# One activation function for all eight FFNs: tanh instead of Silu in four of them, in a hand-planned transformer block

## The chip, the cores and the metric

The kernel runs on one core of one Trainium2 chip. The metric is the device time of one execution in microseconds (us); before the change the median of ten runs is 2534.17 us (2533.23 to 2541.55). The engines are TensorE (PE; its weight loads are listed apart as PEld), VectorE (DVE), ScalarE (ACT), GpSimd (POOL) and SyncE (SP), which issues most DMAs.

## The reference

The input x has 4 sequences of 512 rows of 512 numbers. Four blocks follow each other, each with a layernorm in front and a residual sum behind:

1. attention A: pairwise similarities between all 512 x 512 rows by a small network with two relu layers; the 51 most similar rows are kept for each row; a softmax attention of 32 heads of size 2 over those rows
2. an FFN: `h = silu(gate) * up`, with 2048 gate and 2048 up columns, then a product back to 512
3. attention B: a "difference" attention of 16 heads over all rows, with softmax and projection
4. the same FFN again, with the same weights

`silu(g) = g * sigmoid(g)`, which is the same as `g/2 * (1 + tanh(g/2))`.

## The kernel before, in words

**Work.** The letter and digit in a tile's name tell block and sequence. *Pairs*: for each pair group (1024 in all) DVE, and in a few groups ACT, makes two tiles `m` (line 751 on), PE multiplies them by the second layer's weights into a PSUM bank `z` with 64 columns, ACT takes the relu into `r`, and PE sums over the third layer with 32 columns into `sim` (line 787). For each 128 rows `topk_tile` (line 809) finds the 51 best columns on DVE, gathers their rows with DMAs from POOL, and does the softmax with one large exponential on ACT (`sc`). *FFNs*: f0 to f3 are block 2, e0 to e3 block 4 of the four sequences. `ffn` (line 931) splits float32 into two float16 halves, so that each product is three float16 matmuls. It works in 16 chunks of 128 columns: 24 matmuls give gate and up in two PSUM banks (`e0z` and so on); an activation on ACT and multiplies on DVE give a tile `t`; ACT and DVE split it into two float16 parts for the first 256 rows (`ha`) and the last 256 (`hb`). `ha` goes into the down product at once (`e0a`). `hb` is spilled to HBM (`hk`) and fetched again later (`hc`), when the second half of the down product (`e0b`) runs with its weights `we`. *Attention B* (b0 to b3, line 1017) uses the exponential on ACT for scores and weights.

**The activation before.** Four FFNs (f0, f1, e0, e1) use Silu with a scale column, and one DVE multiply with a scale column. The other four use Tanh and two DVE multiplies with constants. Silu is in another activation table than Exp and Tanh, so a table load stands wherever the two kinds alternate.

**The order.** No instruction is issued while the code above runs: each call of an engine is recorded as a task (`Plan.add`, line 221). `Plan.issue` (line 363) then lists all tasks with a price for each (`cost`, line 148), and a forward and backward pass over the dependencies, the buffers and the engines (`run`, line 261) fixes the order on each engine. In a last pass a shift is added to the rank of each task, by the part of the work that it belongs to (table `SHIFT`, line 53, and `part`, line 73): "e2b" is the late half of e2's down product, "s33" the sums of sequence 3's last 128 rows, "p33v" half of their pair groups. All instructions are issued at line 411, so the profile shows that one line for nearly everything, and work is told by its tiles' names. PSUM has eight banks: seven of the tag `z`, shared by the pair groups, the FFNs and attention B, and one for `sim`. The buffers of tag `fh` (`ha`, `hb`, `hc`) are five.

**The stages.** Pairs of sequence 0 with the preparation of weights; then pairs of 1 to 3 beside f0, b0, e0, f1, b1, e1 and f2 (line 1242); when the pairs are done, b2 beside f3, then b3 and e3 beside e2 (lines 1243 to 1245).

Of the kernel before, what the change touches and what calls it, by code (L numbers as in the profile page):

```python
# [16 lines left out]
AF = mybir.ActivationFunctionType  # L17
ALU = mybir.AluOpType
# [26 lines left out]
def _size(dt):  # L45
# [5 lines left out]


SHIFT = {
    "X0": -16, "X1": -43, "X2": -35, "X3": -35, "a0": -71, "a1": -41, "a2": -39, "a3": -48, "b0n": 10,
    "b0p": -2, "b0q": 16, "b0s": -14, "b0t": -19, "b1n": -40, "b1p": -36, "b1q": -1, "b1s": -34, "b1t": -37,
    "b2n": 13, "b2q": 16, "b2s": -19, "b2t": -20, "b3n": -17, "b3p": 17, "b3q": -9, "b3s": -25, "b3t": -16,
    "c": -67, "e0a": 36, "e0b": 37, "e0n": 18, "e0u": 22, "e0v": 18, "e1a": -13, "e1b": 31, "e1n": -39,
    "e1u": -27, "e1v": -30, "e2a": 25, "e2b": 439, "e2n": -8, "e2u": -11, "e2v": 15, "e3a": 351, "e3b": 380,
    "e3n": 27, "e3u": 63, "e3v": 260, "f0a": 7, "f0b": 4, "f0n": 21, "f0u": 32, "f1a": -14, "f1n": -36,
    "f1u": -19, "f1v": -33, "f2a": 26, "f2b": 13, "f2n": 27, "f2u": 22, "f2v": 20, "f3a": -18, "f3b": -21,  # L60
    "f3n": -39, "f3u": -48, "f3v": -29, "k00": 13, "k01": 24, "k02": 26, "k03": 12, "k10": 50, "k11": 104,
    "k12": 66, "k13": 25, "k20": 28, "k21": 20, "k22": 19, "k23": 76, "k30": 54, "k31": 59, "k32": 70,
    "k33": 84, "p00u": -9, "p00v": -10, "p01u": 17, "p01v": 16, "p02u": 9, "p02v": 7, "p03u": 6, "p03v": 6,
    "p10u": 6, "p10v": 10, "p11u": 3, "p11v": 6, "p12u": -2, "p12v": -1, "p13u": 10, "p13v": 10, "p20u": 8,
    "p20v": 6, "p21u": -1, "p21v": -3, "p22v": -9, "p23u": -18, "p23v": 17, "p30u": 6, "p30v": 3, "p31u": -11,
    "p31v": -9, "p32u": -6, "p32v": 5, "p33u": 8, "p33v": 49, "q0": -17, "q1": 49, "q2": -87, "q3": -94,
    "s00": -358, "s01": -310, "s02": -192, "s03": -207, "s10": -196, "s11": -177, "s12": -37, "s13": 6,
    "s20": 2, "s21": -7, "s22": -2, "s23": 15, "s30": 1, "s31": -13, "s32": -14, "s33": 5, "w": 84, "y0": -82,
    "y1": 272, "y2": -299, "y3": -48,
}  # L70


# [34 lines left out]
class Plan:  # L107
# [9 lines left out]
    DRAIN = 0.1  # L117
    BUSY = 8.0
    READY, MADE = 0.185, 0.17
    LOAD = 1.3  # L120
    PERIOD = 3.41333
    LAG = {"PE": 0.2, "ACT": 0.135, "DVE": 0.12, "POOL": 0.06, "SP": 0.1}

# [24 lines left out]
    def cost(self, key, op, a, k):  # L148


        free = self.free
        if key == "PE":
            n, m = free(a[0]), free(a[1])
            f32 = a[1].dtype == F32
            if op == "transpose":
                return n / 1200 + 0.0025, 128, 0
            w = 32 if m <= 32 else 64 if m <= 64 else 128
            t = (n / 1200 + 0.0027) * 2 if f32 else n / 2400 + 0.0027
            if w < 128:
                t += 0.024 if f32 else 0.012  # L160
            return t, w, (a[0].start_partition() or 0) // w if w < 128 else 0
        if key == "SP":
            return 0.48, 0, 0
        aps = [x for x in a if hasattr(x, "tensor")]
        n = max(free(x) for x in aps)
        ptrs = sum(free(x) == 1 for x in list(a[1:]) + list(k.values()) if hasattr(x, "tensor"))
        psum = any(x.space == PSUM for x in aps)
        if key == "ACT":
            if op == "copy":
                t = 0.04 if psum else 0.08 + (0.29 if n > 600 else 0)  # L170
            elif "accum_out" in k:
                t = 0.33 if psum or n < 100 else 0.187
            else:
                t = 0.16 + (0.04 if ptrs >= 2 else 0.0) if psum else 0.185 + (0.04 if ptrs >= 2 else 0.0 if ptrs else -0.09)

            func = next((x for x in a[1:] if isinstance(x, AF)), None)
            return t + n / 1200, 0, 1 if func in (AF.Exp, AF.Tanh) else 2 if func == AF.Silu else 0
        elif key == "DVE":
            fast = op in ("tensor_scalar", "tensor_copy") and not psum
            if op == "reciprocal":  # L180
                t = 0.055 + n * 0.0064
            elif op in ("max_index", "match_replace"):
                t = 0.673
            elif op == "bn_aggr":
                t = 0.095
            elif op == "tensor_reduce" and not psum and list(a[1].ap)[-1][0] != 1:
                t = 0.06 + n * 0.00173
            elif fast and n == 1:
                t = 0.125 if ptrs >= 2 else 0.065
            else:  # L190
                t = 0.07 + n / (1920 if fast else 960)
                t += 0.06 * (ptrs if fast else op == "scalar_tensor_tensor" and ptrs > 0)
        elif op == "memset":
            t = 0.07 + n / 1200
        else:
            t = {"indirect_dma_start": 1.25, "affine_select": 0.4, "partition_all_reduce": 0.5, "tensor_tensor": 0.3 + 0.2 * n}[op]
        return t, 0, 0
# [63 lines left out]
    def run(self, rank, edges, pre, tags, back=False, stick=0.0):  # L261


        tasks = self.tasks
        n = len(tasks)
# [5 lines left out]
        start = [0.0] * n  # L271
        freed = {m: 0.0 for m in self.tiles}
        now = {k: 0.0 for k in self.kinds}
# [5 lines left out]
            if not waits[i]:  # L279
                heapq.heappush(soon[tasks[i][0]], (0.0, i))  # L280
        order = []
        mode, cols, alle, table = 128, {}, 0.0, None
        win, busy, upto, slow = 0, 0.0, 0.0, False
        P = self.PERIOD

# [16 lines left out]
        while len(order) < n:  # L302
            best = None
            for k in self.kinds:
                if k == "PE" and any(wide.values()) or k != "PE" and able[k]:
                    t = now[k]
# [6 lines left out]
            t, k = best  # L313
# [28 lines left out]
            else:  # L342
                i = heapq.heappop(able[k])[1]
                end = now[k] = t + tasks[i][7]
                if tasks[i][9] and tasks[i][9] != table:
                    if table is not None and not back:
                        end = now[k] = end + self.LOAD
                    table = tasks[i][9]
                if self.xfer[i] and not back:
                    queue = max(queue, t + 1.35) + self.xfer[i]  # L350
                    end = max(queue, t + 1.6 + 1.5 * self.xfer[i])
# [63 lines left out]
def hybrid_block(ctx: ExitStack, tc: tile.TileContext, I, out):  # L415
# [62 lines left out]
    ipw = const("ipw", [128, 5])  # L478
    sc = const("sc", [128, 16])
    s_gu, s_d, s_a, s_p, s_w = (sc[:, i : i + 1] for i in range(5))  # L480
    c_tanh, c_down, c_exp, c_proj, c_kv, w_up, w_dn, c_nexp, c_gate, c_up, c_iexp = (sc[:, i : i + 1] for i in range(5, 16))
    w2s = const("w2s", [128, 2, 64], F16)

    def top(dst, src, n):
# [62 lines left out]
    def prep_scales():  # L547
# [18 lines left out]
            V.tensor_scalar(sc[:, k : k + 1], ipw[:, k : k + 1], 2.0 ** e, None, ALU.mult)  # L566
        p = [pw[:, i : i + 1] for i in range(4)]
        V.tensor_scalar(c_tanh, p[0], 2.0 ** -20, None, ALU.mult)
        V.tensor_scalar(c_gate, p[0], 2.0 ** -19, None, ALU.mult)
        V.tensor_scalar(c_up, ipw[:, 0:1], 2.0 ** -15, None, ALU.mult)  # L570
        V.tensor_scalar(c_down, p[0], p[0], 2.0 ** -16, ALU.mult, ALU.mult)
        V.tensor_scalar(c_down, c_down, p[1], None, ALU.mult)
        V.tensor_scalar(c_proj, p[2], p[3], 2.0 ** -21, ALU.mult, ALU.mult)
# [354 lines left out]
    PARTS = ((0, 0), (0, 1), (1, 0))  # L928


    def ffn(name, X, first=False, late=False, silu=False, store=lambda t: None):
        xt = yield from normed_t(name, X)
        H = S // 2

# [25 lines left out]
        for c in range(NC):  # L960
# [21 lines left out]
                    yield 0.86  # L982
                gu.append(z)
            t = fp.tile([128, S], F32, name=f"{name}t{c}", tag="ft", bufs=2)
            if silu:
                A.activation(t, gu[0], AF.Silu, scale=c_gate)
                V.scalar_tensor_tensor(t, gu[1], c_up, t, ALU.mult, ALU.mult)
            else:

                A.activation(t, gu[0], AF.Tanh, scale=c_tanh)  # L990
                V.scalar_tensor_tensor(t, t, 1.0, gu[0], ALU.add, ALU.mult)
                V.scalar_tensor_tensor(t, gu[1], 2.0 ** -35, t, ALU.mult, ALU.mult)
            ha, hb = (fp.tile([128, 2, H], F16, name=f"{name}h{p}{c}", tag="fh", bufs=FH) for p in "ab")
            for h, ts_ in ((ha, slice(0, H)), (hb, slice(H, S))):
                A.copy(h[:, 0, :], t[:, ts_])
# [169 lines left out]
    def weave(*parts):  # L1165

        at = [p[2] for p in parts]
        live = set(range(len(parts)))
        while live:
            i = min(live, key=lambda j: (at[j], j))  # L1170
            c = next(parts[i][0], None)
            if c is None:
                live.discard(i)
            else:
                at[i] += c / parts[i][1]
                yield c
# [33 lines left out]
    def store(b, t):  # L1210
        SP.dma_start(out[b, t * 128 : (t + 1) * 128], X[b][:, t, :])
# [3 lines left out]
    def start(b):  # L1215
        step_topks(b)
        X[b] = yield from out_a(b)

    def f1(b, **kw):
        return lambda: ffn(f"f{b}", X[b], **kw)  # L1220

    def at(b, **kw):
        return lambda: attn_b(f"b{b}", X[b], **kw)

    def f2(b):
        def g():
            yield from ffn(f"e{b}", X[b], late=b > 1, silu=b < 2, store=lambda t: store(b, t))
        return g

    warm_up()  # L1230
# [4 lines left out]
    main = serial(lambda: pairs(1), lambda: pairs(2), lambda: pairs(3))  # L1235
    side = serial(
        lambda: start(0),
        lambda: weave((f1(0, first=True, silu=True)(), 1, 0), (phase_a(2), 0.2, 20)),
        at(0, first=True),
        lambda: weave((f2(0)(), 1, 0), (phase_a(3), 0.2, 20)),  # L1240
        lambda: start(1), f1(1, silu=True), at(1), f2(1), lambda: start(2), f1(2, late=True))
    emit(weave((main, 1, 0), (side, 1.8, 120)))
    emit(start(3))
    emit(weave((at(2, late=True)(), 1, 0), (f1(3, late=True)(), 1, 20)))
# [57 lines left out]
```

## Time and profile before

| what | us |
|---|---|
| median of ten runs | 2534.17 |
| the profiled execution | 2537.89 |
| its span, first to last instruction | 2536.2 |
| PE busy (records of matmuls) | 2501.5 |
| DVE busy | 2009.4 |
| ACT busy | 1514.3 |
| POOL busy | 976.9 |
| ACT table loads, 19 of 1.283 | 24.4 |
| matmuls of f0's gate and up, first to last start | 503.1 to 657.0 |
| the same of e0, f1, e1 | 980.6 to 1160.7, 1169.1 to 1345.9, 1643.0 to 1779.4 |
| the same of f2, f3, e2, e3 | 1829.0 to 1945.5, 1953.3 to 2128.0, 2222.5 to 2379.6, 2380.5 to 2485.2 |
| pair groups' matmuls, first to last start | 32.9 to 1811.0 |

Times within the span are counted from its first instruction. A line of the list of groups gives engine, operation, what is written and read, the number of instructions, their busy time and the mean of one in ns, and then the idle time of the engine in front of them and who ended it. The granted clock of PE is 0.999 of full speed over the span.

### The profile page before, as it was taken

Reading aid. Unit: us, or ns where it says so; the run is one execution under the profiler, and the core shown is the slowest. Engines: PE = TensorE matmul, PEld = TensorE weight load, DVE = VectorE, ACT = ScalarE, POOL = GpSimd, SP = SyncE. Lnnn points to the kernel's source line nnn. Section 1 sums busy time; section 2 is a strip of 40 time slices with the busy share of each in tenths; the row PEclk is TensorE's granted clock in tenths of the full one; section 3 lists DMA queues with packets and bytes.
Section 4 is the critical chain, followed back from the end, with each engine's and each line's share of the span. In section 5 each row is a group of like instructions: output and inputs, shape, how many; then the busy total and the mean of one; then the engine's idle time right before and its main releaser. Section 6 shows DMA issues by size and latency. Waiting matters only on the chain.

```text
span 2536.2 us, 42662 instructions
## 1 busy us (share of the span) xinstructions
PE 2501.5 (99%) x15044; PEld 1025.5 (40%) x15044; DVE 2009.4 (79%) x5164; ACT 1514.3 (60%) x2831; POOL 976.9 (39%) x847
## 2 busy tenths in 40 slices
PE   8999999999999999999999999999999999999998
PEld 4433343444343334444444333344444443443443
DVE  8889999999899999798686899977856555673531
ACT  6999998656458976443343689643422376586220
POOL 0277767475534155666624234465560000000000
PEclk9999999999999999999999999999999999999999
DMA  5533321157642022436535421045665535523446
GB/s 182 157 105 88 101 61 35 54 162 242 219 133 61 28 64 91 117 115 203 165 94 158 119 55 43 22 115 148 205 212 176 156 115 177 150 93 122 132 143 197
DMA packets 223628, 317.79 MB, mean 125 GB/s; under 512 B 29969, under 2 KB 150865, under 8 KB 222390
## 3 DMA queue, kind: packets, MB, share of 16 engines
q1 hardware_dynamic: 197302, 261.54, 33.1%
q0 software_dynamic: 26112, 53.53, 8.0%
q8 instruction: 118, 1.93, 0.3%
q14 instruction: 96, 0.79, 0.1%
HBM read 263.43 MB, written 51.39 MB: 124 GB/s over the span
## 4 chain that ended last, share of the span: by engine, by line
PE 74%; DVE 17%; DMA 5%; issue 2%; POOL 1%; ACT 1%; SPq 0%; DVEq 0%; POOLq 0%; ACTq 0%
PE z L411 19%; DVE m L411 8%; PE sim L411 6%; PE e0z L411 3%; PE e1z L411 3%; PE e2z L411 3%; PE e3z L411 3%; PE f3z L411 3%; PE f1z L411 3%; PE f2z L411 3%; DVE g L411 3%; PE f0z L411 2%; DVE b1s L411 1%; POOL g L411 1%; DVE b0s L411 1%
## 5 line engine op out<-in xcount | busy, mean ns | idle before, releaser
L411 DVE TENSOR_SCALAR m<-hw 128x512 f32<-128x512 f32 x1888 | 809.0, 482 | 60.6 <-PE z L411 59.5
L411 PE MATMUL z<-m,w2s 128*64 128x512 f16 x5664 | 750.1, 391 | 3.1 <-DVE m L411 1.7
L411 ACT ACTIVATE r<-z,zb 128x512 f32<-128x512 f32 x944 | 612.7, 697 | 221.3 <-PE z L411 159.4
L411 POOL DMA_INDIRECT g<-kv,ix x432 | 497.1, 1151 | 359.7 <-DVE ix L411 208.8
L411 POOL DMA_INDIRECT g<-kv,idx x384 | 469.0, 1221 | 412.7 <-DVE idx L411 194.1
L411 PEld LDWEIGHTS <-w2s 128*64 128x64 f16 x5688 | 315.8, 108 | 491.5 <-issue 226.8
L411 PE MATMUL sim<-r,w 128*32 128x512 f32 x2048 | 274.8, 604 | 0.0
L411 ACT ACTIVATE m<-h 128x512 f32<-128x512 f32 x160 | 107.9, 743 | 5.4 <-PE z L411 5.4
L411 PE MATMUL f3z<-f3xt,f3w 128*128 128x512 f16 x384 | 103.0, 379 | 0.1
L411 PE MATMUL e2z<-e2xt,e2w 128*128 128x512 f16 x384 | 101.5, 379 | 0.0
L411 PE MATMUL f2z<-f2xt,f2w 128*128 128x512 f16 x384 | 98.5, 379 | 0.5 <-DMA f2w<-wf 0.5
L411 PE MATMUL z<-m,h 128*64 128x512 f32 x320 | 98.7, 594 | 0.0
L411 DVE TENSOR_TENSOR g<-g,sc 128x832 f32<-128x832 f32 (+3 forms) x128 | 98.2, 780 | 0.3
L411 PE MATMUL f1z<-f1xt,f1w 128*128 128x512 f16 x384 | 98.3, 379 | 0.0
L411 PE MATMUL f0z<-f0xt,f0w 128*128 128x512 f16 x384 | 90.8, 379 | 0.5 <-ACT f0w L411 0.5
L411 PE MATMUL e0z<-e0xt,e0w 128*128 128x512 f16 x384 | 90.9, 379 | 0.0
L411 PE MATMUL e1z<-e1xt,e1w 128*128 128x512 f16 x384 | 89.5, 379 | 0.0
L411 PEld LDWEIGHTS sim<-r,w 128*32 128x32 f32 x2048 | 41.6, 108 | 115.9 <-issue 95.8
L411 PE MATMUL e3z<-e3xt,e3w 128*128 128x512 f16 x384 | 85.7, 379 | 0.0
L411 DVE MAX8 vm<-sims 128x8 f32<-128x512 f32 x112 | 76.6, 684 | 3.4 <-POOL sims L411 2.9
L411 DVE FIND_INDEX8 ix<-vm,sims 128x8 uint32<-128x512 f32 x112 | 76.3, 681 | 0.0
L411 DVE TENSOR_TENSOR g<-g,q 128x832 f32<-128x832 f32 x64 | 63.9, 999 | 7.1 <-DMA g<-kv,ix 6.1
(643 smaller groups left out, 3776.1 us busy)
## 6 DMA issues: line engine op xcount, KB each, us to landing
f0wr<-wf SPq DMA_DIRECT2D x48, 256.0 KB
wn<-wgu SPq DMA_DIRECT2D x32, 256.0 KB
wf<-f0w SPq DMA_DIRECT2D x16, 512.0 KB
e0w<-wf SPq DMA_DIRECT2D x16, 512.0 KB
f1w<-wf SPq DMA_DIRECT2D x16, 512.0 KB
e1w<-wf SPq DMA_DIRECT2D x16, 512.0 KB
f2w<-wf SPq DMA_DIRECT2D x16, 512.0 KB
f3w<-wf SPq DMA_DIRECT2D x16, 512.0 KB
```

Of the source, the lines that this page charges most:

```text
L411: getattr(eng, op)(*a, **k)
```

## The change

All eight FFNs use the form with Tanh. The two scale columns of the Silu form go. In the planner, the price of a table load goes, with the note of each activation's table. The table of shifts is a new one; since it sets the order of everything, all engines' orders differ, though the matmuls, DMAs and all instructions but those named here are the same in number.

```
 SHIFT = {
-    "X0": -16, "X1": -43, "X2": -35, "X3": -35, "a0": -71, "a1": -41, "a2": -39, "a3": -48, "b0n": 10,
...
+    "X0": -32, "X1": 1, "X2": -17, "X3": 1, "a0": -50, "a1": 75, "a2": -68, "a3": -47, "b0n": -7, "b0p": -12,
...
-    LOAD = 1.3
...
-            func = next((x for x in a[1:] if isinstance(x, AF)), None)
-            return t + n / 1200, 0, 1 if func in (AF.Exp, AF.Tanh) else 2 if func == AF.Silu else 0
+            t += n / 1200
...
-                if tasks[i][9] and tasks[i][9] != table:
-                    if table is not None and not back:
-                        end = now[k] = end + self.LOAD
-                    table = tasks[i][9]
...
-        V.tensor_scalar(c_gate, p[0], 2.0 ** -19, None, ALU.mult)
-        V.tensor_scalar(c_up, ipw[:, 0:1], 2.0 ** -15, None, ALU.mult)
...
-            if silu:
-                A.activation(t, gu[0], AF.Silu, scale=c_gate)
-                V.scalar_tensor_tensor(t, gu[1], c_up, t, ALU.mult, ALU.mult)
-            else:
-
-                A.activation(t, gu[0], AF.Tanh, scale=c_tanh)
-                V.scalar_tensor_tensor(t, t, 1.0, gu[0], ALU.add, ALU.mult)
-                V.scalar_tensor_tensor(t, gu[1], 2.0 ** -35, t, ALU.mult, ALU.mult)
+            A.activation(t, gu[0], AF.Tanh, scale=c_tanh)
+            V.scalar_tensor_tensor(t, t, 1.0, gu[0], ALU.add, ALU.mult)
+            V.scalar_tensor_tensor(t, gu[1], 2.0 ** -35, t, ALU.mult, ALU.mult)
...
-            yield from ffn(f"e{b}", X[b], late=b > 1, silu=b < 2, store=lambda t: store(b, t))
+            yield from ffn(f"e{b}", X[b], late=b > 1, store=lambda t: store(b, t))
...
-        lambda: weave((f1(0, first=True, silu=True)(), 1, 0), (phase_a(2), 0.2, 20)),
+        lambda: weave((f1(0, first=True)(), 1, 0), (phase_a(2), 0.2, 20)),
...
-        lambda: start(1), f1(1, silu=True), at(1), f2(1), lambda: start(2), f1(2, late=True))
+        lambda: start(1), f1(1), at(1), f2(1), lambda: start(2), f1(2, late=True))
```

Some of the shifts that the prediction touches: "e2b" goes from 439 to 46, "e3a" from 351 to 66, "e3b" from 380 to 187, "e3v" from 260 to 46, "s00" from -358 to -691, "s12" from -37 to -6.

## The prediction

> **What bounds the kernel now.** First the page: what each engine does over the whole span, then the slices.
>
> ```profile
> PE 2501.5 (99%) x15044; PEld 1025.5 (40%) x15044; DVE 2009.4 (79%) x5164; ACT 1514.3 (60%) x2831; POOL 976.9 (39%) x847
> ...
> PE   8999999999999999999999999999999999999998
> ...
> DVE  8889999999899999798686899977856555673531
> ACT  6999998656458976443343689643422376586220
> ```
>
> TensorE (PE) looks full, but a record of a matmul lasts longer than its share of the array: the records of one FFN matmul are 379 ns long, and 24 of them in a row take 5.18 us, 0.216 us each. So I price matmuls by the distance of their starts: 0.216 us for a 128x512 f16 matmul, 0.108 for one of a pair group (two column halves work side by side), 0.108 for a record of the pair sums, and so on. All matmuls of the program are then 2317 us of work in a span of 2536.2. The other 219 us are lost. The Trainium skill says the same in "Perfetto Trace Analysis", Identifying the Most-Contended Engine: matmul busy time is a poor measure of the distance to the limit. By that page's other measure, weight loads, PE would be 40% full; no row here supports a reserve that large, and nothing below rests on it.
>
> Next I cut the span where the last pair group ends, at 1811 us, and cut the part before it by stage. The columns are the stretch, its length, and the busy time of PE, weight loads, DVE, ACT and POOL.
>
> ```profile
> 0.00:1811.00 1811.00, 1786.59 (x11593) 710.71 (x11593) 1634.72 (x4215) 1198.32 (x2152) 922.14 (x795) 1.00 0.38 113
> 1811.00:2537.00 726.00, 714.87 (x3454) 314.77 (x3453) 374.69 (x949) 315.97 (x681) 54.76 (x52) 1.00 0.51 156
> ...
> 500.00:660.00 160.00, 159.21 (x914) 65.75 (x914) 146.94 (x329) 93.16 (x157) 97.43 (x80) 1.00 0.65 203
> 980.00:1162.00 182.00, 182.00 (x1104) 74.64 (x1100) 162.71 (x405) 85.21 (x143) 115.90 (x91) 1.00 0.37 111
> 1169.00:1347.00 178.00, 177.27 (x1024) 73.17 (x1023) 129.73 (x288) 69.01 (x113) 79.38 (x76) 1.00 0.50 153
> 1643.00:1781.00 138.00, 138.00 (x780) 58.22 (x780) 105.01 (x237) 53.35 (x93) 85.66 (x76) 1.00 0.44 130
> ```
>
> Before 1811 us PE does 1616.5 us of work (89%) and DVE is busy for 90%; behind it PE does 700.5 us of work in 725 (97%) and DVE is half idle. The last four rows are the stages of the four Silu FFNs (f0, e0, f1, e1): DVE idles there for 13, 19, 48 and 33 us. Between them, at 200 to 520, 760 to 1040 and 1440 to 1640 us, DVE is busy for 319 of 320, 279 of 280 and 199 of 200 us. So PE with its losses is the bound, and DVE is a second one in those three stretches. ACT ends little of the chain of waits (1%).
>
> What is PE's loss made of? Between pair groups (64 columns), pair sums (32) and everything else (128) PE changes its column width. The list of PE's instructions, by start and length:
>
> ```profile
> 1699.26 1.46 PE L411 MATMUL e1a<-e1wd,e1ha 128*128 128x512 f16 x6
> 1700.65 4.26 PE L411 MATMUL z<-m,w2s 128*64 128x512 f16 x36
> 1704.84 5.35 PE L411 MATMUL e1z<-e1xt,e1w 128*128 128x512 f16 x24
> ...
> 1711.33 0.38 PE L411 MATMUL e1z<-e1xt,e1w 128*128 128x512 f16 x1
> 1711.64 1.06 PE L411 MATMUL sim<-r,w 128*32 128x512 f32 x8
> 1712.64 3.63 PE L411 MATMUL e1z<-e1xt,e1w 128*128 128x512 f16 x16
> ```
>
> Six e1a matmuls are 1.30 us, but 1.39 pass until z starts: 0.09 for 128 to 64. 36 z are 3.89 us, 4.19 pass: 0.30 for 64 to 128. In the same way 128 to 32 costs 0.31 - 0.22 = 0.09, and 32 to 128 costs 1.00 - 0.87 = 0.13.
>
> **The change part by part.**
>
> *The order.* No matmul comes or goes. Counting the width changes in the issued order of both programs gives 936 before and 904 after: 7 fewer from 128 to 64, 3 from 64 to 128, 4 from 64 to 32, 11 from 32 to 128, 7 from 128 to 32. By the rows: 14 x 0.09 + 3 x 0.30 + 11 x 0.13 + 4 x 0.30 (64 to 32 has no row of its own; I take its dearest neighbour) = 4.8 us less. Ends: all at 0.09, 2.9; all at 0.30, 9.6.
>
> *The tail.* In the order of before, the late half of FFN e2 (e2b) runs together with that of e3 (e3b) at the end, and both fetch weights and spilled activations at once.
>
> ```profile
> 2485.39 3.19 PE L411 MATMUL e2b<-e2we,e2hc 128*128 128x512 f16 x14
> ...
> 2492.84 1.47 PE L411 MATMUL e2b<-e2we,e2hc 128*128 128x512 f16 x6 [0.81 <-DMA e2hc<-e2hk]
> 2495.33 4.92 PE L411 MATMUL e2b<-e2we,e2hc 128*128 128x512 f16 x22 [1.02 <-DMA e2hc<-e2hk]
> ```
>
> From 2485.4, when e3z is done, 192 matmuls (41.5 us) take until 2532.0: 5.1 us are lost, and the DMA engines are 98% busy at 2492 to 2500. In the new order e2b is done long before; behind e3z stand 30 e3a and 96 e3b, 27.2 us. Their first fetch (e3hc0) stands in SP's queue behind the last spill (e3hk15). In before that spill was issued 2.5 us after e3z, the next fetch 0.6 later, and PE had it 4.2 us after that: 7.3 in all, of which the 30 e3a cover 6.5. So 0.8 is left to wait and about 4 us are won. Ends: 5.1 won; or 4.0 more lost, which is what the f0b matmuls waited for DMAs.
>
> *DVE.* In 64 chunks one multiply with a scale column (0.746 us, rows of e0t to f1t) becomes two without (0.688 each, rows of e2t to f3t): 0.63 x 64 = 40 us more, 10.1 in each FFN. In f1 and e1 the idle 48 and 33 us hide it. In f0 10.1 meets 13 idle, and e0's first 60 us lie in a full stretch (about 5 of 16 chunks, 3 us). I take 4. Ends: 0, and all 40. Two dropped one-column scales are nothing.
>
> *ACT.* Tanh lasts as long as Silu (0.69 us, rows of e0t and e2t). 18 of 19 table loads go.
>
> ```profile
> 1819.33 0.58 ACT L411 CAST f2xt<-f2t 128x512 f16<-128x512 f32 x1 [4.44 <-PE f2t L411]
> 1819.93 1.28 ACT L411 ACT_TABLE_LOAD   x1
> 1821.23 1.56 ACT L411 ACTIVATE sc<-sc 128x1632 f32<-128x1632 f32 x1
> ```
>
> That is 18 x 1.28 = 23 us of ACT, which is 60% busy and about half busy where the loads stand. I take 1 us won; ends 0 and 23. The Trainium skill ("ScalarE: Activation LUTs", What ACT_TABLE_LOAD costs) adds a drain of about 1.38 us to each load; by it ACT would win 48 us. The rows show 0.02 us on either side of the load and no drain, so the rows decide.
>
> *PSUM.* The gate's bank is now held through a DVE multiply behind the activation, and the up bank for one multiply more: some 0.8 us per chunk, out of seven banks that the pair groups share. Before shows Tanh FFNs only where no pair group is left. Ends: 0, and 64 x 0.8 = 51 us; I take 1, as PE ran e3z at 105 us busy of 105 in that form.
>
> Sum: -4.8 - 4 + 4 - 1 + 1 = -4.8, so 5 us less. The profiled execution took 2537.89 us (span 2536.2) and would take 2533; it lies 3.7 over the median, so against 2534.17 I forecast **2529**.
>
> **The rivals.**
>
> *A: DVE becomes the bound until the pairs end (slower).* In the new order the last pair group stands after 1579 us of PE work, 37 earlier, with the same pair work and up to 40 us more on DVE. So DVE has 1675 us to do where PE alone would need about 1811 - 37 - 5 = 1769: a share of 94.7%, against 90.3% now. Behind the pairs there are 738 us of work, at 725/700.5 and less the tail's 4: 760. At a share of 94% the sum is 1782 + 760 = 2542, at 93% 1801 + 760 = 2561; it is slower than now below 94.4%. For it: it must nearly reach over 1800 us what only the full stretches show. Against: those three stretches, 800 us together, show 99.6%, and the idle time is in the FFN stages, where the new work is.
>
> *B: the new order fills PE better (faster).* Before the pairs end PE loses 194 us; 856 width changes at 0.15, between the prices above, are 128. The other 66 are waits. If the order saves a quarter, 16 us, the time is 2513. I cut both orders at every 59th pair group and took for each piece the larger of PE's work with 0.2 per width change and DVE's work: before's pieces come out to about 3 us, and the new order is 2 us shorter; with longer and shorter pieces between 14 shorter and 16 longer. So A and B are both open.
>
> *C: nothing.* The saved changes of width were time in which DVE caught up, and the tail waits elsewhere: 2534.
>
> **How the numbers follow.** Forecast (2522 to 2536) 0.50, of it 0.27 faster, 0.22 same, 0.01 slower; A 0.27 (0.25 slower, 0.02 same); B 0.15 faster; C 0.08 (0.05 same, 0.03 slower). Within 0.2% means within 5.1 us, about what measuring this kernel can tell. Faster 0.42, same 0.29, slower 0.29. The range reaches into B and A: 2512 to 2548. The far ends (51 for PSUM, 40 for DVE) would need every chunk to stall PE, against the idle time shown.
>
> **What would show it.** One table load; DVE busy near 2049; PE's end 27 to 29 us after the last e3z, without e2b; the last pair group near 1775 us. If that comes after 1790 with DVE idle below 5% until then, A holds; if before 1760, B. Waits of the first pair matmul for a freed z bank would show the PSUM price. If e3b waits for e3hc by more than 2 us, the tail's step is wrong.

## The result, and the profile after

The changed kernel takes **2546.22 us** (median of 9 runs, 2541.59 to 2550.73) against 2535.64 us of the kernel before in the same comparison: the ratio is 1.0042, interval 1.0033 to 1.005. So it is slower by 0.42%, about 10.6 us. Measured twice more among the experiments, the ratio is 1.0028 [1.0018, 1.0038] and 1.0047 [1.0033, 1.0061].

The page of the changed kernel: busy time of each engine, the slices, the chain of waits by engine.

```profile
PE 2500.1 (98%) x15044; PEld 1020.9 (40%) x15044; DVE 2048.0 (81%) x5226; ACT 1496.6 (59%) x2813; POOL 960.5 (38%) x847
...
PE   8999999999999999999999999999999999999999
...
DVE  8899999999999999798897899988766565564422
ACT  7998988655458985343443489753321475586211
...
PE 71%; DVE 14%; issue 6%; DMA 5%; POOL 2%; ACT 1%; SPq 1%; DVEq 0%; POOLq 0%; ACTq 0%
```

DVE has 38.6 us more (2009.4 to 2048.0) and ACT 18 instructions fewer (2831 to 2813, the table loads): both as counted beforehand. In the chain, "issue" has 6% instead of 2%: in the list of the chain's pieces that is one piece, from 3.09 us for 100.10, where the trail is lost. So the chain says nothing of the first 100 us, and nothing here shows where 10 us went. Nor do the stages, in the same columns as those of before (stretch, length, busy PE, weight loads, DVE, ACT, POOL, granted clock, DMA share, GB/s). The last pair group now ends at 1781.5.

```profile
0.00:1781.50 1781.50, 1749.09 (x11423) 689.34 (x11424) 1642.49 (x4194) 1172.42 (x2115) 886.63 (x773) 1.00 0.37 110
...
1781.50:2541.00 759.50, 751.02 (x3622) 331.61 (x3621) 405.51 (x1033) 324.13 (x699) 73.85 (x75) 1.00 0.53 160
```

DVE idles for 7.8% ahead of the last pair group. And of its 38.6 us only 7.8 lie there (1642.5 against 1634.7): a part of e1 and what follows moved behind the pairs.

What finds the loss is a count. I give each matmul the price of the prediction (0.216 us for a 128x512 f16, and so on), add them up in PE's order, and note when a given amount of this work is done. Each column is the profiled execution of one kernel, minus that of before, in us; e1 to e14 are experiments below.

```
work done   after   e9 (after)  e16 (after)    e1     e3     e4    e11    e13    e14
   24 us     +6.4      +6.7       +6.4        +3.1   +0.5   +6.6   +5.3  +10.0    0.0
  100        +7.9      +8.5       +9.0        +3.6   +0.5   +8.6   +6.4  +11.4    0.0
  200        +9.8     +10.6      +11.0        +5.2   +0.7  +11.2   +9.2  +14.3   +0.1
  600       +10.3     +10.4      +11.3        +8.7   +1.8   +9.3   +8.5  +21.3   -0.2
 1000       +10.0     +10.0      +10.5        +7.3   +5.1   +9.0   +9.1  +25.8   +0.2
 1600        +9.9      +7.3      +12.3        +6.1   +5.2   +9.6   +9.1  +25.4   +0.3
 2250       +11.9      +8.4      +11.7        +6.3   +4.6  +12.5   +8.4  +24.8   +0.3
 2316 (all)  +7.0      +3.8       +7.5        +1.3   +1.9  +10.4   +6.5  +19.9   -4.5
```

The last row is smaller than the differences of medians by 3.7, since the profiled execution of before lay 3.7 over its median: 7.0 + 3.7 = 10.7, measured 10.6; 3.8 + 3.7 = 7.5 for e9, measured 7.4. The three columns of the changed kernel agree: **6.4 to 6.7 us are lost before 24 us of work are done**, 1.5 to 2.6 more until 100 (124 us into the span of before), between 0 and 4 from there to 2250, and the tail gives 4 to 5 back. About 2 of that belong to the one profiled execution of before: e3, e4 and e11 have the tail of before, and their columns fall there by 1.9 to 2.7 as well. The first 44 us of the changed kernel hold no FFN and few pair groups, so neither the FFNs' multiplies nor the tail can be the cause there.

So look at PE's list of instructions from 15 to 43 us, first of before:

```profile
15.57 2.84 PE L411 MATMUL hp<-xnT,wa 128*128 128x512 f32 x6 [0.88 <-ACT xnT L411]
...
22.22 3.03 PE L411 MATMUL qp<-wa,xnT 128*128 128x192 f32 x10
...
26.15 2.12 PE L411 MATMUL qp<-wa,xnT 128*128 128x192 f32 x12
...
29.11 0.54 PE L411 MATMUL zp<-hw,w2s 128*64 128x256 f16 x6 [0.40 <-DVE hw L411]
29.84 1.36 PE L411 MATMUL xt<-ident,xl 128*128 128x128 f32 x8 [0.19 <-ACT xl L411]
...
32.88 4.74 PE L411 MATMUL z<-m,w2s 128*64 128x512 f16 x40
37.54 1.07 PE L411 MATMUL sim<-r,w 128*32 128x512 f32 x8
```

and then of the changed kernel:

```profile
15.25 0.59 PE L404 MATMUL qp<-wa,xnT 128*128 128x192 f32 x2 [0.40 <-ACT xnT L404]
16.08 2.54 PE L404 MATMUL qp<-wa,xnT 128*128 128x192 f32 x14 [0.24 <-DVE xnT L404]
...
19.60 2.87 PE L404 MATMUL qp<-wa,xnT 128*128 128x192 f32 x16 [0.43 <-ACT xnT L404]
22.30 3.60 PE L404 MATMUL hp<-xnT,wa 128*128 128x512 f32 x8
27.87 0.46 PE L404 MATMUL top<-diag,ones 128*128 128x128 f32 x2 [1.97 <-DVE ln_1rs L404]
33.46 0.85 PE L404 MATMUL zp<-hw,w2s 128*64 128x256 f16 x6 [5.13 <-DVE hw L404]
34.11 6.30 PE L404 MATMUL z<-m,w2s 128*64 128x512 f16 x41
40.33 2.76 PE L404 MATMUL sim<-r,w 128*32 128x512 f32 x8
```

Everything in the pairs hangs on one chain of sequence 0: hp (PE), its maximum hm (DVE, PE's top, DVE), ht (ACT), hw (DVE), zp, z. In before, hp starts at 15.6 and PE fills the chain's wait with the products qp. The shift "q0" goes from -17 to -377 in the change: now all 32 qp records stand ahead of hp, hp starts at 22.3, and PE has nothing left for the wait: 1.97 and 5.13 us idle. DVE's list adds to it. In before the statistics of sequence 1 (ln_1st) are done when hp ends, and hm's first reduction follows hp at once; the end of that layer norm stands behind it:

```profile
15.57 1.28 DVE L411 BATCH_NORM_STATS2 ln_1st<-x 128x6 f32<-128x512 f32 x2
...
20.22 0.69 DVE L411 TENSOR_REDUCE hm<-hp 128x1 f32<-128x512 f32 x1
...
29.25 0.89 DVE L411 TENSOR_SCALAR m<-hw 128x512 f32<-128x512 f32 x2
...
30.43 2.48 DVE L411 TENSOR_SCALAR m<-hw 128x512 f32<-128x512 f32 x6
```

In the changed kernel hm starts 0.7 us after hp, because the statistics are in front of it, and they had waited for x:

```profile
23.88 1.29 DVE L404 BATCH_NORM_STATS2 ln_1st<-x 128x6 f32<-128x512 f32 x2 [0.95 <-DMA x<-x]
...
25.16 1.25 DVE L404 BATCH_NORM_STATS2 ln_1st<-x 128x6 f32<-128x512 f32 x2
...
26.55 0.66 DVE L404 TENSOR_REDUCE hm<-hp 128x1 f32<-128x512 f32 x1
...
32.12 1.28 DVE L404 TENSOR_TENSOR hw<-ht 128x1024 f16<-128x1024 f32 x1
```

They waited because the fetch of sequence 1's rows is issued 10 us later than in before (SyncE's list, before and then the changed kernel):

```profile
5.34 0.43 SPq L411 DMA_DIRECT2D x<-x  x1
```

```profile
15.69 0.39 SPq L404 DMA_DIRECT2D x<-x  x1
```

Something else differs too: the granted clock is 0.5 for 6.83 us from 29.8, a stretch that begins inside the wait, and the first 41 z take 6.2 us where 40 took 4.7.

So there were four theories. **Opening**: the chain's late start, without a filler, costs most of the 10 us. **Clock**: the half clock behind the wait is what costs. **DVE**: the two multiplies cost, more than the 4 us that I gave them. **Middle**: the new order costs where pairs and FFNs interleave.

### The profile page after: what moved, and what is told of

Its sections match the earlier page's. It is cut to its first block, busy times and chain, and to the rows that moved or that the text cites. A ratio compares the mean times of both kernels' runs of the same rounds, so it can differ in the third digit from the quotient of the medians.

```text
span 2543.1 us, 42644 instructions
## 1 busy us (share of the span) xinstructions
PE 2500.1 (98%) x15044; PEld 1020.9 (40%) x15044; DVE 2048.0 (81%) x5226; ACT 1496.6 (59%) x2813; POOL 960.5 (38%) x847
## 4 chain that ended last, share of the span: by engine, by line
PE 71%; DVE 14%; issue 6%; DMA 5%; POOL 2%; ACT 1%; SPq 1%; DVEq 0%; POOLq 0%; ACTq 0%
PE z L404 19%; PE sim L404 7%; DVE m L404 6%; PE e0z L404 3%; PE f1z L404 3%; PE e1z L404 3%; PE e2z L404 3%; PE e3z L404 3%; PE f3z L404 3%; PE f2z L404 3%; DVE g L404 2%; POOL g L404 2%; DVE b0s L404 1%; PE f0z L404 1%; PE e2a L404 1%
## 5 line engine op out<-in xcount | busy, mean ns | idle before, releaser
L404 POOL DMA_INDIRECT g<-kv,ix x432 | 482.4, 1117 | 456.8 <-DVE ix L404 320.6
L404 PE MATMUL e3z<-e3xt,e3w 128*128 128x512 f16 x384 | 98.4, 379 | 0.0
L404 DVE TENSOR_TENSOR g<-g,sc 128x416 f32<-128x416 f32 (+3 forms) x128 | 97.5, 781 | 0.2
L404 PE MATMUL f1z<-f1xt,f1w 128*128 128x512 f16 x384 | 90.8, 379 | 0.0
```

Of the source, the lines that this page charges most:

```text
L404: getattr(eng, op)(*a, **k)
```

## The experiments

Kernels of one comparison shared a chip and its runs of before. Where a variant is set against the changed kernel of another comparison, the changed kernel's own spread counts: it lay 7.4, 10.6 and 10.9 us over the before beside it. The ratios are not quotients of the medians and can differ from them by some 0.1% (e7: 1.0009, where the medians give 1.0001).

**e1: q0 set back.** In the table of the changed kernel:

```
-    ... "q0": -377,
+    ... "q0": -17,
```

> The kernel after the change with one shift put back: q0 (the products q, k, v of sequence 0) from -377 to -17, as before. The order of the last 12,000 of 13,502 matmuls stays. Theory 'opening' (the new order puts these products ahead of the product hp that the first pair groups wait for, and the 6 to 9 us lost there by the time PE has done 128 us of work stay lost to the end): 2540, at most 2542, ratio to before about 1.0015; PE has done 24 us of work at about 38 us from the start, as before the change (37.3), and not at 43.7. Rival 'DVE' (the 40 us more on DVE are what is paid, and a late opening is made up for, since pair groups wait for DVE anyway): no change against the changed kernel, 2546, ratio 1.004.

Measured: 2539.16 us, ratio 1.002 [1.0009, 1.0032]: 3.7 over before, where the changed kernel lay 7.4 to 10.9 over it, so 4 to 7 us are won by the medians, 2 to 7 by the ratios; the intervals of e1 and of one of the three (e9) overlap widely. The loss at 100 us of work is 3.6 instead of 7.9 to 9.0. What is left of it: PE waits 5.87 us for hw, because ln_1st still stands ahead of it on DVE and waits for x, whose fetch is issued at 15.8 here too:

```profile
24.01 1.29 DVE L404 BATCH_NORM_STATS2 ln_1st<-x 128x6 f32<-128x512 f32 x2 [0.69 <-DMA x<-x]
```

Its column then rises from 3.6 at 100 us of work to 8.7 at 600, where the changed kernel's rise by 1.9 to 2.4; no run shows why.

**e2: Silu in the new order.** In the four FFNs, exchanged at the place where the instructions are issued, so that no order changes; in effect:

```
-            A.activation(t, gu[0], AF.Tanh, scale=c_tanh)
-            V.scalar_tensor_tensor(t, t, 1.0, gu[0], ALU.add, ALU.mult)
-            V.scalar_tensor_tensor(t, gu[1], 2.0 ** -35, t, ALU.mult, ALU.mult)
+            A.activation(t, gu[0], AF.Silu, scale=c_gate)
+            V.scalar_tensor_tensor(t, gu[1], c_up, t, ALU.mult, ALU.mult)
```

> The kernel after the change, every engine's order kept, but with Silu and one DVE multiply in f0, e0, f1, e1 as before the change; 19 table loads come back and DVE loses 40 us of work. Theory 'opening': the form costs next to nothing, so 2546 within 3, ratio 1.003 to 1.005. Rival 'DVE': the 10 us come back, 2536, ratio 1.000; the last pair group ends some 10 us earlier than in the changed kernel (1781).

Measured: 2544.73 us, 1.0035 [1.0022, 1.0047]. That is 9.3 over before, inside the 7.4 to 10.9 of the changed kernel: no worth of the form is shown in the new order.

**e3: Tanh in the old order**, the reverse edit in before. 

> The kernel before the change, PE's order kept, but with Tanh and two DVE multiplies in f0, e0, f1, e1 (the first one put into DVE's order three DVE instructions behind the activation, or just ahead of the second); one table load. Theory 'opening': 2536 within 4, ratio 0.999 to 1.002. Rival 'DVE': 2546, ratio 1.004 or more.

Measured: 2540.2 us, 1.002 [1.0011, 1.0028], 4.7 us more than before on that chip (2535.46). The count puts 3.6 of it between 800 and 1000 us of work, where e0 begins in a full stretch of DVE, and about 1 in f0; f1 and e1 show none.

**e4: the old tail.** The changed kernel with e2b and the e3 shifts of before ("e2b" 46 to 439 and so on); only the order behind the 12,782nd of 13,502 matmuls differs. 

> The kernel after the change with the shifts of e3 and e2b put back (e2b 439, e3a 351, e3b 380, e3n 27, e3u 63, e3v 260), which changes the order behind the 12,782nd matmul alone. By the prediction's step on the tail it is 4 to 5 us slower than the changed kernel: 2550.5, ratio 1.006, with waits of e2b for its fetches. If the new tail won nothing: 2546, ratio 1.004.

Measured: 2549.37 us, 1.0054 [1.0042, 1.0066]: 13.9 over before, so 3 more than the slower two measurements of the changed kernel (10.6 and 10.9) and 6.5 more than the fastest; the intervals overlap. In the profiles its end lies at +10.4 where the changed kernel's lies at +7.0.

**e5 to e8** drew a chip on which before itself takes 2560.89 us, 1% more than on the others, and the kernels profiled there show losses strewn over the span. The changed kernel wasn't run there, so these runs decide little.

**e5: idle matmuls, first try.** 22 matmuls of ones by the identity behind sequence 0's second top:

```
+            plan.swap[i] = [(op, a, k)] + 22 * [("matmul", (zw[:, 128:256], ones, ident), dict(start=True, stop=True))]
```

> The kernel after the change with 22 idle float32 matmuls (ones times identity, 128x128, about 0.21 us each; their result is never read) right behind the small matmul 'top' of sequence 0, where PE is idle for 5.1 us. Everything else stays. They take no time from anybody. In the changed kernel the granted clock fell to 0.5 from 29.8 to 36.6 us, and 41 matmuls of pair groups then took 6.2 us instead of 4.5, and 8 of pair sums 2.7 instead of 1.0. Theory 'clock' (half of the opening's loss is the slow clock behind the idle time): no 0.5 in the opening, PE has done 24 us of the program's work 3 us earlier than 43.7, and the time is 3 us lower: 2543, ratio 1.003. Rival 'order alone' (the wait for the chain behind hp is everything): 2546, and the clock falls at the same place.

Measured: 2583.21 us, 1.0088 [1.0066, 1.0111]. The edit missed its aim, as PE's list shows:

```profile
28.60 5.08 PE L406 MATMUL top<-ident,ones 128*128 128x128 f32 x44
38.82 0.85 PE L406 MATMUL zp<-hw,w2s 128*64 128x256 f16 x6 [5.14 <-DVE hw L406]
```

The idle matmuls (two records each) write the bank that DVE's reduction of top reads, so it waited for them too: they pushed the whole chain back by 5 us, and the wait of 5.14 came behind them unchanged.

**e6: nine opening shifts of before** (q0, a0, a1, q1, y0, y1, s00, p00u, p00v) in the changed kernel. 

> The kernel after the change with all shifts of the opening put back (q0, a0, a1, q1, y0, y1, s00, p00u, p00v). The matmuls then stand as before the change up to sequence 1's preparation; they are another order up to the 6500th, and that of the changed kernel behind. Theory 'opening': PE has done 100 us of work at 124 us, as before the change, and the time is at most that of the run with q0 alone, 2536 to 2539, ratio 1.000 to 1.0015. Rival 'the rest of the order': the early gain is lost again by 600 us, 2542 or more, ratio 1.0025.

Measured: 2589.47 us, 1.0099 [1.0077, 1.012]. Not what the opening theory wanted. zp comes early, at 27.65, but sequence 1's transposes xt stand ahead of z and wait 2.18 us for xl, z starts at 37.9 (32.9 in before), and the loss is 5.2 at 100 us of work. What is lost later on that chip, with many stretches of half clock, I leave open.

**e7: before, with "e2b" 46 alone.** 

> The kernel before the change with one shift of the changed one: e2b from 439 to 46, so that the late half of e2's down product is done before the end. The order changes behind the 12,878th matmul alone. By the tail step and by the run with the old tail (3 us): 2532.5, ratio 0.9988; matmuls behind the last e3z end within 28 us of it. If the old tail cost nothing in its own place: 2535.5, ratio 1.000.

Measured: 2561.09 us, 1.0009 [0.9992, 1.0026]: no gain shown, though PE ends 27.6 us after the last e3z, as expected.

**e8: before, with Tanh in f0, f1, e1 and Silu in e0.** 

> The kernel before the change, PE's order kept, with Tanh and two DVE multiplies in f0, f1 and e1 but Silu left in e0. With Tanh in all four, 3.6 of the 4.7 us came between 925 and 1143 us, in e0, whose first part lies in a stretch where DVE is always busy. Theory 'DVE where it is full': 2537, ratio 1.0005, and no loss there. Rival 'every FFN alike' (banks held longer, or a fixed cost per chunk): three quarters of 4.7, 2539, ratio 1.0015.

Measured: 2566.1 us, 1.002 [1.0007, 1.0034]. The interval leaves out the 1.0005 of the theory, barely, and holds the 1.0015 of the rival. On this chip, where this kernel's runs spread over 17 us, that is weak, but it speaks against the place in e0 as the cause, not for it.

**e9: the changed kernel again**, on a chip where before takes 2534.68. 

> The changed kernel once more, unaltered, so that the kernels beside it have a baseline on the same chip. Every theory expects the ratio of before, 1.004, again: about 10 us more than before. If the ratio lies under 1.002 or over 1.006, the loss depends on the chip, and the earlier differences between variants carry that as an uncertainty.

Measured: 2542.06 us, 1.0028 [1.0018, 1.0038]. So 7 to 11 us is the size, not 10.6 exactly.

**e10: the wait filled, second try**, in front of zp, into columns of its bank that it does not use:

```
+        if b == 0:
+            i = len(plan.tasks) - 6
+            _, _, op, a, k = plan.tasks[i][:5]
+            plan.swap[i] = 20 * [("matmul", (zp[:, 256:384], ones, ident), dict(start=True, stop=True))] + [(op, a, k)]
```

> The changed kernel with 20 idle 128x128 f32 matmuls (ones by the identity, 0.23 us each by the earlier run with idle matmuls, so about 4.6 us) into unused columns of zp's bank, directly in front of sequence 0's zp, so that they fill the 5.13 us in which TensorE waits for hw, and no step of the chain waits for them. Theory that the half clock follows that wait: no 0.5 clock behind 33 us in its profile, z's first 41 in about 4.6 us instead of 6.2, sims 1.0 instead of 2.7, and 3 to 4 us less than the unaltered changed kernel. Rival, that the half clock has another cause (a rise of load, or the table of the start): the 0.5 clock stands where it stood, and the time is that of the unaltered kernel within 1 us. If the 2 us wait ahead of top sets it, the 0.5 clock stays for one stretch of 3.41 us.

Measured: 2546.29 us, 1.0045 [1.0032, 1.0059]; spans of the profiled executions 2540.6, and 2540.0 of e9 beside it; by the medians it is 4.2 slower than e9. The windows of e9, and then of e10 (the third number from the end is the granted clock):

```profile
30.72:34.13 3.41, 0.39 (x4) 0.35 (x6) 3.13 (x11) 3.38 (x5) 0.00 (x0) 0.56 0.15 53
34.13:37.55 3.42, 3.42 (x21) 2.09 (x19) 3.42 (x10) 3.42 (x9) 0.00 (x0) 0.50 0.01 2
```

```profile
30.72:34.13 3.41, 2.68 (x25) 2.59 (x25) 3.15 (x11) 3.38 (x5) 0.00 (x0) 1.00 0.42 155
34.13:37.55 3.42, 3.06 (x24) 1.23 (x25) 3.37 (x9) 3.42 (x7) 0.00 (x0) 1.00 0.01 2
```

The half clock is gone. PE's list of e10 behind it:

```profile
28.77 4.63 PE L406 MATMUL zp<-ident,ones 128*128 128x128 f32 x40
34.13 0.55 PE L406 MATMUL zp<-hw,w2s 128*64 128x256 f16 x6 [0.73 <-DVE hw L406]
34.72 1.27 PE L406 MATMUL z<-m,w2s 128*64 128x512 f16 x7
36.30 4.77 PE L406 MATMUL z<-m,w2s 128*64 128x512 f16 x34 [0.31 <-DVE m L406]
41.00 2.69 PE L406 MATMUL sim<-r,w 128*32 128x512 f32 x8
```

At full clock the first 41 z still take 6.3 us and the sims 2.7. PE waits for the masks m: DVE, busy for 3.37 of 3.42 us, makes one per 0.41 us (six in 2.48 us, in before's list at 30.43), and three z use one (5664 z, 1888 m in the list of groups), so 41 z at that pace take 5.6. In before z starts 3.6 us after the masks (32.88 against 29.25) and finds some ready; that is why 40 z take 4.7 us there. The half clock does slow PE while it lasts: in e9 z starts every 0.21 us up to 37.7, while e10 has one every 0.13. But e9 then catches up at full clock, and its 41st z starts at 40.58, that of e10 at 40.66. So the clock theory falls here: what the half clock held back was made up, since the masks set the pace of the whole stretch. My expectation of 3 to 4 us was wrong.

**e11: the shift in before**, "q0" from -17 to -377 and nothing else. By the traces the order of PE differs in the first third only. 

> The kernel before, with one shift of the changed one: that of sequence 0's q and kv products, -17 to -377, so that they stand ahead of hp. Silu, two thirds of the order and the tail are those of before. Theory that the order of the opening costs the time: hw about 4 us later than in before, TensorE waits over 4 us for it, a half clock behind that, and 5 to 8 us more than before. Rival, that the loss comes from the order of the middle: within 2 us of before.

Measured: 2544.85 us (2544.19 to 2545.25), 1.0038 [1.0025, 1.0052]: 10.2 more, above the 5 to 8 expected, and no less than the whole change on that chip (7.4, e9). Its list of PE:

```profile
19.23 1.88 PE L411 MATMUL hp<-xnT,wa 128*128 128x512 f32 x4
...
27.00 0.46 PE L411 MATMUL top<-diag,ones 128*128 128x128 f32 x2 [2.65 <-DVE pw L411]
32.69 0.85 PE L411 MATMUL zp<-hw,w2s 128*64 128x256 f16 x6 [5.24 <-DVE hw L411]
```

The same wait as in the changed kernel; and its column in the count goes from 5.3 to 9.2 within 200 us of work and stays at 8 to 9 until the tail. The one shift moves more than qp: the fetch of sequence 1's rows is issued at 14.5 instead of 5.3, ln_1st stands ahead of hm on DVE (22.8 to 25.5), and the transposes xt and hp of sequence 1 come ahead of nearly all z. So e11 shows what this shift costs, not which of these things costs it.

**e12: q0 set back, and Silu in f0 and e0** of the changed kernel. 

> The changed kernel with that shift of the opening set back (as in e1) and Silu with one multiply in f0 and e0, Tanh in f1 and e1, in the order of the changed kernel. Theory that opening and DVE's work are separate terms: 7 us less from the opening and 1 to 3 from the form, so 8 to 10 less than the unaltered changed kernel, about the time of before; with the tail of the changed kernel it may come out up to 2 us under it. Rival, that the two hide behind one another (DVE's load in f0 only costs because the opening was late): no more than the 7 us of e1.

Measured: 2540.12 us, 1.0015 [1.0006, 1.0024], runs from 2533.65 to 2543.55. That is 2 less than the unaltered kernel beside it, where 8 to 10 were expected, though its profiled execution took only 2534.24. By the ratios (1.0028 and 1.0015) it is some 3 less, either way well under the sum of 7 from the opening and 1 to 3 from the form. The spread, wider than before's own, is unexplained.

**e13: the chain first**, that is three shifts of before in the changed kernel:

```
-    ... "a1": 75, ... "q0": -377, ... "y1": -18
+    ... "a1": -41, ... "q0": -17, ... "y1": 272
```

> The changed kernel with three shifts of before: q0 -17, a1 -41, y1 272. hp and the chain behind it then stand ahead of the q and kv products as in before, and the statistics of sequence 1 stand behind hw on VectorE. Theory that the chain's late start is the loss of the opening: zp starts at 28 to 30 us (33.5 in the changed kernel), TensorE's work of 100 us is done within 2 us of before, and the kernel takes 7 to 9 us less than the changed one. Rival, that the loss lies in the number of matmuls that can fill the waits and not in the chain: the work of 100 us is done 5 us or more after before, and no more is won than the 7 us of e1.

Measured: 2555.75 us, 1.008 [1.0066, 1.0094], 10 more than the changed kernel beside it (e16), and 17 to 19 off the expectation.

```profile
14.68 3.87 PE L404 MATMUL hp<-xnT,wa 128*128 128x512 f32 x8
...
29.87 0.85 PE L404 MATMUL zp<-hw,w2s 128*64 128x256 f16 x6 [6.86 <-DVE ln_1rs L404]
...
36.58 1.12 PE L404 MATMUL xt<-ident,xl 128*128 128x128 f32 x4 [3.01 <-ACT xl L404]
...
43.37 3.35 PE L404 MATMUL z<-m,w2s 128*64 128x512 f16 x28
```

The chain does come early: zp at 29.87, as expected. But "a1" -41 put sequence 1's transposes xt ahead of z, they wait for sequence 1's normed rows (xl), and z starts only at 41.9. Nor did the shift of y1 do what it was meant to: sequence 1's rows are still fetched at 15.1, and its statistics still stand ahead of hw on DVE:

```profile
23.28 1.29 DVE L404 BATCH_NORM_STATS2 ln_1st<-x 128x6 f32<-128x512 f32 x2 [0.77 <-DMA x<-x]
...
28.49 1.32 DVE L404 TENSOR_TENSOR hw<-ht 128x1024 f16<-128x1024 f32 x1
```

So here an early chain gained nothing, since what stands ahead of z in PE's fixed order is late. My theory was too narrow: the chain's start alone does not decide. So it was in e6, which had this shift of a1 too. And the opening is less than half of this kernel's loss: its column has 11.4 at 100 us of work and 25.8 at 1000; the rest is unexplained.

**e14: the new tail in before**, e2b and the five e3 shifts of the changed kernel; the order differs behind the 12,748th matmul. 

> The kernel before with the changed kernel's shifts of e2b, e3a, e3b, e3n, e3u, e3v; the order differs from before only behind the 12,748th of 13,502 matmuls. Theory of the tail (e2b out of the end): 3 to 5 us less than before, PE's end 27 to 29 us after the last e3z. Rival, that the tail's gain belongs to the changed kernel alone: within 1.5 us of before.

Measured: 2532.64 us, 0.999 [0.9981, 0.9999], 1.9 less than before, under the expected 3 to 5: the one version that beats both kernels, if barely. Its end, in PE's list:

```profile
2495.24 4.91 PE L411 MATMUL e3z<-e3xt,e3w 128*128 128x512 f16 x22
2499.99 6.64 PE L411 MATMUL e3a<-e3wd,e3ha 128*128 128x512 f16 x30
2506.46 21.07 PE L411 MATMUL e3b<-e3we,e3hc 128*128 128x512 f16 x96
```

No wait is left: PE ends 27.4 us after the last e3z.

**e15: e13 with Silu in f0 and e0.** 

> As e13, and Silu with one multiply in f0 and e0. If the terms opening, DVE and tail add up, 2531 to 2535, that is up to 3 us under before; if they hide behind one another, as e13 within 1 us.

Measured: 2551.83 us, 1.007 [1.0056, 1.0084]. The 2531 to 2535 fell with e13; against e13 the form is worth 3.9 us here; the intervals overlap.

**e16: the changed kernel beside them.** 

> The changed kernel unaltered, beside the three on the same chip: 7 to 11 us more than before, by both earlier measurements.

Measured: 2545.44 us, 1.0047 [1.0033, 1.0061], 10.9 more than before.

## Why the prediction was wrong

The time lies inside the range, but I forecast 5 us less, and it is 7 to 11 more. By the steps:

- **The order** failed: "14 x 0.09 + 3 x 0.30 + 11 x 0.13 + 4 x 0.30 = 4.8 us less". It priced a new order of all engines by one property, the number of width changes. Of those 4.8 us no run shows anything. The sum had no term for the opening, though the diff shows "q0" going to -377, and PE's list of before shows qp filling the wait behind hp from 22.2 to 28.7. The term that was missing is 2 to 7 (q0 set back in the changed kernel, e1) to 10 (q0 alone in before, e11); the count puts 6.4 to 6.7 of the changed kernel's loss and 5.3 of e11's before 24 us of work. The order of the two programs, read for the first 50 us alone, would have shown it: 32 qp ahead of hp, nothing behind it; from the end of hp to zp the chain takes 9 us in before (20.2 to 29.1), and it would have stood bare.
- **The tail** held in kind and was sized too high: PE ends 27.2 us after the last e3z, in the forecast 27 to 29, and e3b waits nowhere.

```profile
2506.84 4.91 PE L404 MATMUL e3z<-e3xt,e3w 128*128 128x512 f16 x22
2511.59 6.64 PE L404 MATMUL e3a<-e3wd,e3ha 128*128 128x512 f16 x30
2518.07 20.88 PE L404 MATMUL e3b<-e3we,e3hc 128*128 128x512 f16 x96
```

  The 4 us measure 1.9 in before (e14, interval 0.3 to 4.8); e7, which moves e2b alone, shows no gain; e4 gives 3 to 6.5, with overlapping intervals. The term was read from one execution: from the end of the last e3z to PE's end before's profile has 46.4 us, with 4.1 of waits for DMAs; e3, e11 and e4, with the same tail, have 43.7 to 44.6, with 1.7 to 2.1.
- **DVE** held in size: 4 us, of it most in e0's first part; measured 4.7 in before's order (e3, interval 2.8 to 7.1), by the count of one execution in the places named (about 1 in f0, 3.6 where e0 begins), nothing shown in the new order (e2), 3.9 in that of e13. That the place in e0 is the reason is not shown; e8 speaks weakly against it.
- **ACT**: the loads went. No run takes them alone: e2 puts them back and takes DVE's second multiplies away, and the two together show no change. **PSUM**: not tried by itself; e3 has it together with DVE's work and without the table loads, and all that costs 4.7, far from 51.
- **Rival A** gave 2542, near the time, but it is not what happened: the last pair group ends at 1781.5, not after 1790, DVE idles there for 7.8%, not under 5%, and only 7.8 us of DVE's new work lie ahead of it where A counted 40. **B**, before 1760, fell too.
- The 3.7 us by which before's profiled execution lay over its median were taken off rightly, but some 2 of them were waits in the tail, which the tail's 4 us counted as a gain once more.

The parts tried alone in before give 10.2 + 4.7 - 1.9 = 13.0 (q0's shift, DVE with PSUM and ACT, tail), the whole change 7.4 to 10.9. The 2 to 6 between may be the saved width changes (4.8 predicted) or parts that hide behind one another; no run tells which. The **middle** had no run of its own; the count leaves it 0 to 4. Which part of the 10 us of e11 belongs to hp's late start, which to the missing filler, and which to the late fetch of sequence 1's rows, is open as well: no run moves one of them alone.

**What the half clock costs.** In the changed kernel the granted clock is 0.5 for 6.83 us from 29.8, which is 1.5 us after the wait of 5.13 us began; with that wait filled (e10) it is 1.00 there. The Trainium skill ("TensorE: Matmul & The Clock Gate", Part 1: The HAM clock gate) says that TensorE falls to half clock after an idle window of about 3.4 us. The traces agree only in part: from the end of hp to 29.8 TensorE worked for 0.46 of 3.9 us, but in before the clock is 0.5 for 3.41 us from 21.3, where no wait of TensorE nearby is longer than 1.5 us. Under "HAM oscillation" the page prices the loss as the throttled time by one minus the ratio; by that, 3.4 us here, an estimate. e10 differs: with the half clock removed nothing was won, since the masks set the pace.

## What to carry to other kernels

When a change brings a new order, walk the opening first, instruction by instruction on every engine: find the chain that the bulk of the work hangs on, and ask what each engine does during its waits and whether that work is still behind the chain in the new order. Ask the same of the DMA queue: one shift in the table also put a fetch 9 us later (e11). The time that e11 lost in the first 200 us of work stayed lost to the end, though TensorE idled later too. And size a term for waits from more than one execution: the tail's 4 us were 1.9. Last, find the place of a loss by counting work done against time in both traces before trying causes: shares of busy time showed none of this, and the half clock, which began inside the wait, was a symptom.

## What the runs showed of the hardware

Two things that I had not expected. A granted clock of 0.5 for 6.83 us cost nothing that can be measured: TensorE fell behind while it lasted and caught up behind it, because the masks came more slowly than TensorE works at full clock (e9 and e10). And chips differ by more than this change: before took 2534.57 to 2535.64 us in four comparisons and 2560.89 in the fifth, on a chip measured once, 1% more, so variants measured on different chips can be compared only by their ratio to before, and even this ratio was not the same for the unaltered kernel (1.0028 to 1.0047).
